# A selective-scan, attention and feed-forward kernel: the back stage's transposes, D*u, mean and the projection's z, put together in another way

## The chip, the cores and the metric

The kernel runs on one core of one Trainium2 chip. A core has TensorE (PE in the profile, with its weight loads as PEld), VectorE (DVE), ScalarE (ACT), GpSimd (POOL) and SyncE (SP), whose queue issues all of this kernel's DMAs. The metric is the device time of one execution in microseconds. Three runs of the kernel before gave 11664.7, 11660.78 and 11644.77 us; the median is 11660.78 us.

## The reference

The input is x, 8 images of 96 channels by 64 x 64 pixels (L = 4096). What is computed for each image:

```
xh  = layernorm over channels(x)
xz  = xh @ in_proj_w.T ;  xi, z = the two halves, 192 channels each
xi  = silu(depthwise 3x3 convolution(xi))
xs  = xi in four orders of the pixels (rows, columns, both reversed)
delta, B, C = projections of xs ;  A = -exp(A_log)
h_t = exp(delta_t*A)*h_(t-1) + delta_t*u_t*B_t ;  y_t = C_t.h_t + D*u_t
y   = sum of the four orders, back in pixel order
y   = layernorm over 192 channels(y) * silu(z)
out = y @ out_proj_w.T + x
```

After it come linear attention without a softmax (6 heads) and a feed-forward part with weights and activations rounded to eight bits. The layer norm over channels of the first line is (x - mean)/sqrt(var + 1e-5); the one of y is the one that the change rearranges.

## The kernel before

The images go in four pairs. Channels are on partitions; 4096 pixels are cut into 8 chunks of F = 512. The 192 channels are held as two halves of DIM = 96 (index g).

For every pair there are these stages, each a generator that gives control back with `yield`; `together` (line 880) interleaves two of them in program order:

- `project` (238): channel norm of x, then, per chunk, matmuls with winT: `pm` (128 channels of xi, line 287), `pl` (the other 64, written to the rows `lo` of image b, line 294) and `pz` twice (two halves of z, 96 channels each, line 303). ScalarE adds the bias into the padded images `y` (288, 295), and takes silu of z into `zt` (307), stored by one DMA to `zs` in DRAM (310).
- `convolve`, `gates`, `prepare` (313 to 439): the 3x3 convolution, silu, and the scan's inputs.
- `scan` (442): the recurrence, with an order of the instructions that is written out by hand (`manual_schedule`). Its results go to `ys` in DRAM.
- `back` (692): 16 chunks per pair (8 chunks of 2 images). For each: loads of z (`z3`, 731), u (`ut`, 733), x (`xr`, 738) and of the four orders of y (`yk`, 744 and 750, six DMAs, 1.5 MB); two adds that fold four orders into two (754 on VectorE, 755 on GpSimd); the transposes; the norm of y; the gate with z (796, 799); the output projection `po` (802) plus x into `ta` (806), which is stored to `t1`. `heads` (703) takes `ta` of the chunk before: a norm (`ncp`, `nvp`, lines 680 and 684, `tn` 687), keys and values `pk` (712), and their products `pm` (721).
- `tail` (829): attention's output and the feed-forward part.

`back` of one pair runs together with `project` of the next (16 steps against 34); for the last pair it runs alone. `tail` runs together with `convolve` and `prepare` of the next pair. `scan` runs by itself. Outside `scan`, the order in each engine's queue, SP's included, is set when the kernel is built, by the framework's planner, from program order, from buffers that come free and from its own estimates of durations. On the chip each engine takes its queue in order. Tile pools have a fixed number of buffers (`bk` 2, for yk, z3, ut, xr and others); a load waits until the buffer's last reader is done.

The scan leaves y with pixels on partitions, 24 channels (NE) side by side for each of 8 blocks, so a transpose on TensorE is a matmul with the data as weights and an identity as the moving operand. In `back`, half g of a chunk is put into the PSUM bank `py` in this way: first one matmul with `dpad[:, g]`, a diagonal with the sum of D, applied to u (line 759); then, for two orders k, four pixel groups j and four blocks e, one matmul each with 24 weight columns, written to rows 32e to 32e+23 (768). The channels so lie in four groups of 24 with 8 empty rows between. `py` is copied out to `yt` (773 on VectorE, 775 on ScalarE), and `c192` (identity minus the mean's 1/192, in the same padded layout) centres both halves with two matmuls each into two banks `yc` (781). ScalarE squares them (784), `j192` averages the squares into `yv` (788), and `rsqrt` is an Ln and an Exp on ScalarE (189, 190). Every float32 matmul appears as two matmul instructions in the profile.

Of the kernel before, what the change touches and what calls it, by code (L numbers as in the profile page):

```python
# [10 lines left out]
F32 = mybir.dt.float32  # L11
# [8 lines left out]
DIM = 96  # L20
# [32 lines left out]
def vss_attn_ffn(ctx: ExitStack, tc: tile.TileContext, a: dict):  # L53
# [26 lines left out]
    c192 = const.tile([128, 2, DIM], F32, name="c192")  # L80
    nc.vector.memset(c192, 0.0)
    for e in range(4):
        rows = slice(NE * e, NE * e + NE)
        nc.sync.dma_start(c192[32 * e : 32 * e + NE, 0], a["c192"][rows, 0, 0:DIM])
        nc.sync.dma_start(c192[32 * e : 32 * e + NE, 1], a["j192"][rows, 0, 0:DIM])
    nc.vector.tensor_scalar(c192[:, 1], c192[:, 1], -1.0, None, ALU.mult)
# [38 lines left out]
    inz = cut("inz", a["inb"][:, 1].unsqueeze(2), 1)  # L125
# [9 lines left out]
    dpad = const.tile([DIM, 2, 128], F32, name="dpad")  # L135
    nc.vector.memset(dpad, 0.0)
    for g in range(2):
        for e in range(4):
            nc.vector.tensor_scalar(
                dpad[:, g, 32 * e : 32 * e + NE], ident[0:DIM, NE * e : NE * e + NE],  # L140
                dsum[:, g : g + 1], None, ALU.mult,
            )
# [95 lines left out]
    def project(pair, zs, ybuf, p1, tmp, ps):  # L238
# [5 lines left out]
        nc.sync.dma_start(winT, a["winT"])  # L244
        for b in range(2):
# [36 lines left out]
            lo = slice(64 * b, 64 * b + 64)  # L282
            for c in range(NCH):
# [10 lines left out]
                nc.tensor.matmul(pl[lo], winT[:, 128:DI], xt[:, cs], start=True, stop=True)  # L294
# [5 lines left out]
                zt = tmp.tile([DIM, 2, F], F32, name="zt")  # L300
                for g in range(2):
                    pz = ps.tile([128, F], F32, name="pz", tag="fps")
                    nc.tensor.matmul(
                        pz[:DIM], winT[:, DI + g * DIM : DI + (g + 1) * DIM], xt[:, cs],
                        start=True, stop=True,
                    )
# [385 lines left out]
    def back(pair, ys, us, zs, t1, tn, tmp, psy, psc, psm, ps):  # L692
# [34 lines left out]
            for c in range(NCH):  # L727
                cs = bass.ts(c, F)
                for b in range(2):
                    zt = tmp.tile([DIM, 2, F], F32, name="z3")  # L730
                    nc.sync.dma_start(zt, zs[b, :, :, cs].rearrange("g p l -> p g l"))
# [22 lines left out]
                    nc.vector.tensor_tensor(yk[:, 0], yk[:, 0], yk[:, 2], ALU.add)  # L754
                    nc.gpsimd.tensor_tensor(yk[:, 1], yk[:, 1], yk[:, 3], ALU.add)  # L755
                    yt = tmp.tile([128, 2, F], F32, name="yt")
                    for g in range(2):
                        py = psy.tile([128, F], F32, name="py")
                        nc.tensor.matmul(py, dpad[:, g], ut[:, g], start=True, stop=False)  # L759
                        for k in range(2):  # L760
                            for j in range(4):
                                for e in range(4):
                                    o = py[32 * e : 32 * e + NE]
                                    if k % 2 == 0:
                                        o = o.rearrange("p (n j) -> p n j", j=4)[:, :, j]
                                    else:
                                        o = o.rearrange("p (g j w) -> p g j w", g=2, j=4)[:, :, j]
                                    nc.tensor.matmul(  # L768
                                        o, yk[:, k, 4 * g + e, NE * j : NE * j + NE], ident,
                                        start=False, stop=(k + j == 4),  # L770
                                    )
# [299 lines left out]
```

## Time and profile before

| | |
|---|---|
| median of three runs | 11660.78 us (11644.77 to 11664.7) |
| span of the profiled execution | 11664.0 us |
| TensorE busy | 8587.3 us (74%) |
| VectorE busy | 8817.1 us (76%) |
| ScalarE busy | 6931.4 us (59%) |
| GpSimd busy | 7968.6 us (68%) |
| DMA | 2095.89 MB, mean 180 GB/s |

The profile gives one execution. The page holds the busy time of each engine, the span in 40 slices, the DMA queues, the chain of work that ended last and the costliest groups of instructions. The trace answers more: the windows view gives each engine's busy time, the granted TensorE clock (1.00 is full) and the DMA share in any stretch; the timeline lists instructions in order of time; the groups view gives count, busy time and mean duration by line. The printed end of a matmul is modelled and has the depth of the pipeline in it.

### The profile page before, as it was taken

To read this page: it belongs to the slowest core of one execution; us is meant where nothing else is said; L and a number is where in the kernel's file an instruction comes from. 1 tells how busy PE (TensorE), PEld (TensorE's weight loads), DVE (VectorE), ACT (ScalarE), POOL (GpSimd) and SP (SyncE) were. 2 spreads that over 40 slices of the span, in tenths; PEclk is the share of its full clock that TensorE was granted. 3 is DMA by queue.
4 is the path that set the end of the run, shared out by engine and by line. 5 is a ranking of instruction groups with operands and counts; after the bars stand their busy time and mean duration, and the time that the engine had idled before them with its cause. 6 is when DMAs were issued, how large, how long until landed. Compare 5 with 4: busy or idle time off the path is not lost. (4 is left out here: it accounts for less than half of the span.)

```text
span 11664.0 us, 386998 instructions
## 1 busy us (share of the span) xinstructions
PE 8587.3 (74%) x170112; PEld 5661.1 (49%) x170112; DVE 8817.1 (76%) x6465; ACT 6931.4 (59%) x12227; POOL 7968.6 (68%) x2770
## 2 busy tenths in 40 slices
PE   7866666679876666767996666667898666666687
PEld 2255555554325555554422555555442355555542
DVE  5489999963659889995366999999445699999922
ACT  3666666654556666664455666666446566666623
POOL 0489999960259999994025999999303699999910
PEclk8678888889768888888976888888996688888896
DMA  2988888875488888886558888888636888888852
GB/s 82 233 200 203 197 200 200 199 165 135 134 200 198 198 191 199 205 198 152 125 152 203 198 198 201 199 202 199 148 98 181 205 202 203 201 194 200 191 133 65
DMA packets 1362204, 2095.89 MB, mean 180 GB/s; under 512 B 372484, under 2 KB 1012997, under 8 KB 1357701
## 3 DMA queue, kind: packets, MB, share of 16 engines
q1 hardware_dynamic: 1360516, 2071.13, 74.5%
q8 instruction: 1335, 21.87, 0.9%
q14 instruction: 353, 2.88, 0.1%
HBM read 1606.70 MB, written 464.01 MB: 178 GB/s over the span
## 5 line engine op out<-in xcount | busy, mean ns | idle before, releaser
L597 DVE TENSOR_TENSOR_SCAN h<-da,dbu 128x774 f32<-128x774 f32 x4096 | 7027.0, 1760 | 669.3 <-ACT da L586 449.9
L561 POOL TENSOR_TENSOR dbu<-dut,bc 128x1536 f32<-128x1536 f32 x2048 | 7084.1, 3508 | 615.6 <-ACT dbu L558 460.9
L586 ACT ACTIVATE da<-da 128x768 f32<-128x768 f32 x4092 | 3255.2, 798 | 2184.3 <-PE da L579 2145.6
L615 PE MATMUL yp<-h,cw 128*32 128x48 f32 x131072 | 3133.4, 246 | 1088.4 <-issue 1072.9
L579 PE MATMUL da<-dm,aw 128*128 128x128 bf16 x24576 | 2503.4, 251 | 1469.1 <-DVE h L597 1145.0
L615 PEld LDWEIGHTS yp<-h,cw 128*32 128x32 f32 x131072 | 2543.3, 155 | 1641.3 <-issue 1377.0
L579 PEld LDWEIGHTS <-aw 128*128 128x128 bf16 x24576 | 1844.6, 111 | 1785.9 <-issue 1467.5
L515 ACT ACTIVATE cw<-bc,blk 128x512 f32<-128x512 f32 x2048 | 1474.7, 721 | 251.0 <-DMA bc<-cs 222.1
L755 POOL TENSOR_TENSOR yk<-yk 128x768 f32<-128x768 f32 x64 | 117.2, 1831 | 1262.2 <-DMA yk<-ys 870.9
L433 POOL TENSOR_TENSOR dp<-rest,dp 128x512 bf16<-128x512 f32 x384 | 473.9, 1237 | 674.5 <-ACT dp L432 673.2
L623 ACT ACTIVATE yev<-yp 128x384 f32<-128x384 f32 x1024 | 503.4, 492 | 257.8 <-PE yp L615 256.8
L431 DVE TENSOR_TENSOR rest<-delta,dp 128x512 f32<-128x512 f32 x384 | 335.3, 876 | 420.4 <-ACT dp L430 420.2
L410 PE MATMUL pq<-S,dtw 12*128 12x512 f32 x768 | 559.0, 837 | 111.2 <-ACT delta L414 92.6
L796 DVE SCALAR_TENSOR_TENSOR g<-yc,c_onw,yrs 96x512 f32<-96x512 f32 x128 | 89.9, 742 | 472.1 <-ACT yrs L190 472.1
L868 POOL TENSOR_TENSOR ot<-t,y 96x512 f32<-96x512 f32 x64 | 101.8, 1590 | 483.7 <-DVE y L866 391.2
L558 ACT COPY dbu<-h 128x12 f32<-128x12 f32 x1984 | 407.9, 206 | 0.0
L432 ACT ACTIVATE dp<-rest 128x512 bf16<-128x512 f32 x384 | 240.2, 628 | 276.5 <-DVE rest L431 275.8
L410 PEld LDWEIGHTS pq<-S,dtw 12*128 12x128 f32 x768 | 155.2, 238 | 497.0 <-ACT delta L414 270.8
L682 ACT ACTIVATE nsq<-ncp 96x512 f32<-96x512 f32 x128 | 75.7, 592 | 523.6 <-PE ncp L680 496.8
L390 POOL COPY u<-xi 128x512 f32<-128x512 f32 x96 | 100.0, 1054 | 350.6 <-ACT xi L356 296.6
L768 PEld LDWEIGHTS py<-ident,yk 128*24 128x24 f32 x8192 | 229.2, 107 | 224.4 <-issue 166.9
L768 PE MATMUL py<-ident,yk 128*24 128x128 f32 x8192 | 311.9, 286 | 28.3 <-DVE yk L754 22.0
(136 smaller groups left out, 6764.8 us busy)
## 6 DMA issues: line engine op xcount, KB each, us to landing
dut<-du SPq DMA_DIRECT2D x1024, 768.0 KB
dm<-dl SPq DMA_DIRECT2D x512, 576.0 KB
dl<-dp SPq DMA_DIRECT2D x256, 384.0 KB
dm<-dl SPq DMA_DIRECT2D x512, 192.0 KB
ys<-yev SPq DMA_DIRECT2D x1024, 96.0 KB
du<-du SPq DMA_DIRECT2D x256, 256.0 KB
bc<-bs SPq DMA_DIRECT2D x512, 128.0 KB
bc<-cs SPq DMA_DIRECT2D x512, 128.0 KB
```

What stands on the lines that cost most here:

```text
L410: nc.tensor.matmul(pq, dtw[64:76, k, T], S[64:76], start=True, stop=True)
L431: nc.vector.tensor_tensor(rest, d, dp[:, :, 0], ALU.subtract)
L433: nc.gpsimd.tensor_tensor(dp[:, :, 2], rest, dp[:, :, 1], ALU.subtract)
L515: nc.scalar.activation(cw[i % 2][:, :, :, m, :].rearrange("p z j t -> p (z j) t"), bc[i][:, 1].rearrange("p z (j t) -> p (z j) t", j=NB), ...
L558: nc.scalar.copy(start, segs(hs[s - 1][:, :, r])[:, :, :, 1 if back else TC])
L561: nc.gpsimd.tensor_tensor(segs(t)[:, :, :, 1:], dut[g // 2][:, NI * (r % 2) : NI * (r % 2) + NI, :].unsqueeze(1) .to_broadcast([128, 2, NI ...
L579: nc.tensor.matmul(e[:, i], aw[k, r][:, i, z, :], dm[s // 2][:, NI * r + i, bass.ts(c % 2, TC)], start=True, stop=True,)
L586: nc.scalar.activation(e, e, AF.Exp)
L597: nc.vector.tensor_tensor_scan(hs[s][:, w, r][:, d], da[p % 3][:, o : o + W6][:, d], dbu[4 * s + r][:, w][:, d], 0.0, ALU.mult, ALU.add,)
L615: nc.tensor.matmul(y[32 * q : 32 * q + 32, 2 * NE * i : 2 * NE * i + 2 * NE] .rearrange("p (j r i) -> p i j r", j=2, r=NR), w[:, z, :, t], ...
L623: nc.scalar.activation(yev[s][:, :, o : o + 8, :].rearrange("p j i e -> p i j e"), y[:, 0 : 16 * NE].rearrange("p (i j e) -> p i j e", j=2 ...
L768: nc.tensor.matmul(o, yk[:, k, 4 * g + e, NE * j : NE * j + NE], ident, start=False, stop=(k + j == 4),)
```

## The change

The edits, in words:

1. After the adds, which now write into a new tile `yd` in the order (k, j, block, channel), the 96 channels of a half lie side by side. One matmul with 96 weight columns replaces four with 24: 16 per chunk instead of 64. The channels come out on rows 0 to 95 with no gaps.
2. `dpad` goes. VectorE's scalar_tensor_tensor reads `py` from PSUM and writes `yt = u*dsum + py`, in place of the copies.
3. The mean of y is one pair of matmuls with `j192` into one bank `mean`; VectorE subtracts it from both halves of `yt` in place, and ScalarE squares `yt`. `c192` goes, and so do the small loads and VectorE instructions that made `c192` and `dpad` at the start.
4. In `project`, the first 64 channels of z ride with the 64 rows of `pl` in one 128-column matmul (for the second image by a small extra tile `swap` with the columns exchanged), and the other 128 channels are one `pz` matmul: three matmuls per chunk instead of four. `zt` is stored by two DMAs. `zs` is laid out [2, 192, L].
5. `py` has two banks instead of one, the centring's pool one instead of two.

```diff
             lo = slice(64 * b, 64 * b + 64)
+            hi = slice(64 - 64 * b, 128 - 64 * b)
+            mixed = swap if b else winT[:, 128 : DI + 64]
...
-                nc.tensor.matmul(pl[lo], winT[:, 128:DI], xt[:, cs], start=True, stop=True)
+                nc.tensor.matmul(pl, mixed, xt[:, cs], start=True, stop=True)
...
-                zt = tmp.tile([DIM, 2, F], F32, name="zt")
-                for g in range(2):
-                    pz = ps.tile([128, F], F32, name="pz", tag="fps")
-                    nc.tensor.matmul(
-                        pz[:DIM], winT[:, DI + g * DIM : DI + (g + 1) * DIM], xt[:, cs],
-                        start=True, stop=True,
-                    )
+                zt = tmp.tile([128, 2, F], F32, name="zt")
+                pz = ps.tile([128, F], F32, name="pz", tag="fps")
+                nc.tensor.matmul(pz, winT[:, DI + 64 :], xt[:, cs], start=True, stop=True)
+                for r, g, v in ((hi, 0, pl), (slice(0, 128), 1, pz)):
                     table("silu", lambda: nc.scalar.activation(
-                        zt[:, g], pz[:DIM], AF.Silu, bias=inz[:, g]
+                        zt[r, g], v[r], AF.Silu, bias=inz[r, g : g + 1]
                     ))
-                nc.sync.dma_start(zs[b, :, :, cs].rearrange("g p l -> p g l"), zt)
+                nc.sync.dma_start(zs[b, 0:64, cs], zt[hi, 0])
+                nc.sync.dma_start(zs[b, 64:DI, cs], zt[:, 1])
...
-                    nc.vector.tensor_tensor(yk[:, 0], yk[:, 0], yk[:, 2], ALU.add)
-                    nc.gpsimd.tensor_tensor(yk[:, 1], yk[:, 1], yk[:, 3], ALU.add)
-                    yt = tmp.tile([128, 2, F], F32, name="yt")
+                    yd = tmp.tile([128, 2, 4, 8 * NE], F32, name="yd")
+                    for k, eng in ((0, nc.vector), (1, nc.gpsimd)):
+                        eng.tensor_tensor(
+                            yd[:, k].rearrange("p j (s e) -> p s j e", s=8),
+                            yk[:, k].rearrange("p s (j e) -> p s j e", j=4),
+                            yk[:, k + 2].rearrange("p s (j e) -> p s j e", j=4), ALU.add,
+                        )
+                    yt = tmp.tile([DIM, 2, F], F32, name="yt")
                     for g in range(2):
                         py = psy.tile([128, F], F32, name="py")
-                        nc.tensor.matmul(py, dpad[:, g], ut[:, g], start=True, stop=False)
                         for k in range(2):
                             for j in range(4):
-                                for e in range(4):
-                                    o = py[32 * e : 32 * e + NE]
...
-                                    nc.tensor.matmul(
-                                        o, yk[:, k, 4 * g + e, NE * j : NE * j + NE], ident,
-                                        start=False, stop=(k + j == 4),
-                                    )
-                        if g == 0:
-                            nc.vector.tensor_copy(yt[:, g], py)
-                        else:
-                            nc.scalar.activation(yt[:, g], py, AF.Copy)
-                    yc = []
+                                o = py[:DIM]
...
+                                nc.tensor.matmul(
+                                    o, yd[:, k, j, DIM * g : DIM * g + DIM], ident,
+                                    start=(k + j == 0), stop=(k + j == 4),
+                                )
+                        nc.vector.scalar_tensor_tensor(
+                            yt[:, g], ut[:, g], dsum[:, g : g + 1], py[:DIM], ALU.mult, ALU.add
+                        )
+                    mean = psc.tile([128, F], F32, name="mean")
+                    for g in range(2):
+                        nc.tensor.matmul(
+                            mean[:DIM], j192, yt[:, g], start=(g == 0), stop=(g == 1)
+                        )
                     sq = tmp.tile([DIM, 2, F], F32, name="ysq", bufs=1)
                     for g in range(2):
-                        p = psc.tile([128, F], F32, name="yc")
-                        for i in range(2):
-                            nc.tensor.matmul(
-                                p[:DIM], c192[:, i ^ g], yt[:, i], start=(i == 0), stop=(i == 1)
-                            )
-                        nc.scalar.activation(sq[:, g], p[:DIM], AF.Square)
-                        yc.append(p)
+                        nc.vector.tensor_tensor(yt[:, g], yt[:, g], mean[:DIM], ALU.subtract)
+                        nc.scalar.activation(sq[:, g], yt[:, g], AF.Square)
...
-                            gt, yc[g][:DIM], onw[:, g], rs, ALU.mult, ALU.mult
+                            gt, yt[:, g], onw[:, g], rs, ALU.mult, ALU.mult
...
-                        pool("bk", 2), pool("bky", 1, space=PSUM), pool("bkc", 2, space=PSUM),
+                        pool("bk", 2), pool("bky", 2, space=PSUM), pool("bkc", 1, space=PSUM),
```

More of the change, by code (lines that the diff above doesn't have):

```diff
@@ L124, in vss_attn_ffn @@
     woT = cut("woT", a["woT"], DIM)
-    inz = cut("inz", a["inb"][:, 1].unsqueeze(2), 1)
+    inz = const.tile([128, 2], F32, name="inz")
+    for o in (0, 64):
+        nc.sync.dma_start(inz[o : o + 64, 0:1], a["inb"][0:64, 1, 0:1])
+    nc.sync.dma_start(inz[0:64, 1:2], a["inb"][64:128, 1, 0:1])
+    nc.sync.dma_start(inz[64:128, 1:2], a["inb"][0:64, 1, 1:2])
     outb = load("outb", [DIM, 1])
@@ L244, in project @@
         nc.sync.dma_start(winT, a["winT"])
+        swap = p1.tile([DIM, 128], F32, name="swap")
+        nc.sync.dma_start(swap[:, 0:64], a["winT"][:, DI : DI + 64])
+        nc.sync.dma_start(swap[:, 64:128], a["winT"][:, 128:DI])
         for b in range(2):
```

27 lines of the change are left out of this document (6 added, 21 removed).

## The prediction

> **What bounds the kernel now.** First I read the page's parts 1 and 2, then where the changed lines run, then who is late there. No engine fills the span (VectorE 76%, TensorE 74%): the span is four scans of about 1900 us, in which the changed lines do not run, and the stages between them. By first and last starts in the trace, the back stage beside the next pair's projection runs from 2514 to 2944, 5384 to 5818 and 8240 to 8671 us (three "merged" stages, some 430 us each), the back stage alone from 11100 to 11486, and the first projection alone from 47 to 219. The rest, tail, convolution, preparation and scans, has no changed line. So the question is what ends last in these five stretches. The view of windows, for a merged stage past its start and for the back stage alone (columns: length, then busy us of PE, PEld, DVE, ACT, POOL, then granted clock, DMA share, GB/s):
>
> ```profile
> 5457.00:5795.00 338.00, 325.37 (x2531) 153.39 (x2529) 106.99 (x154) 165.39 (x259) 23.51 (x13) 1.00 0.58 136
> 11205.00:11287.00 82.00, 72.18 (x694) 36.88 (x687) 22.41 (x31) 23.35 (x40) 7.21 (x4) 1.00 0.64 143
> ```
>
> TensorE is the bound of the merged stage: 325 of 338 us at full clock, while ScalarE has 49%, VectorE 32%, GpSimd 7% and the DMA engines 0.58. Alone, the back stage has TensorE at 88%: nearly the bound, with some chain in it. So the next view is the timeline of TensorE over one chunk of the back stage alone (start, us, line):
>
> ```profile
> 11318.23 1.72 PE L768 MATMUL py<-ident,yk 128*24 128x128 f32 x54
> 11319.88 3.67 PE L781 MATMUL yc<-yt,c 128*96 128x512 f32 x8
> 11323.39 1.94 PE L788 MATMUL yv<-ysq,j 96*96 96x512 f32 x4
> 11325.17 1.02 PE L759 MATMUL py<-ut,dpad 96*128 96x512 f32 x2
> 11326.12 1.07 PE L768 MATMUL py<-ident,yk 128*24 128x128 f32 x32
> 11328.87 1.96 PE L802 MATMUL po<-g,c_woT 96*96 96x512 f32 x4 [1.67 <-DVE g L799]
> ...
> 11331.61 0.84 PE L768 MATMUL py<-ident,yk 128*24 128x128 f32 x18
> 11332.38 1.10 PE L684 MATMUL nvp<-nsq,c_j 96*96 96x512 f32 x2
> 11333.41 0.63 PE L768 MATMUL py<-ident,yk 128*24 128x128 f32 x14
> 11334.84 1.13 PE L759 MATMUL py<-ut,dpad 96*128 96x512 f32 x2 [0.80 <-DVE yt L773]
> 11335.90 0.40 PE L768 MATMUL py<-ident,yk 128*24 128x128 f32 x2
> 11336.23 1.57 PE L712 MATMUL pk<-c_wkv,tn 97*128 97x192 f32 x8
> ```
>
> The printed length of a group has the pipeline's end in it, so I cost a group from its start to the next group's start. The period is 20.86 us (the x54 group returns at 11339.09). In it are 3.51 us of L781, 0.95 + 1.06 of L759, and 128 instructions of L768 in 1.65 + 1.07 + 0.77 + 0.63 + 0.33 and 0.35 (a group of 8 at 11338.23) = 4.80 us. Two waits are visible: 1.67 us for the gate's g, and 0.80 us because the one py bank is still being copied out. The last view is the same timeline in the merged stage, at the projection:
>
> ```profile
> 5569.58 1.07 PE L294 MATMUL pl<-xt,winT 96*64 96x512 f32 x2
> 5570.59 1.13 PE L759 MATMUL py<-ut,dpad 96*128 96x512 f32 x2
> 5571.55 1.88 PE L303 MATMUL pz<-xt,winT 96*96 96x512 f32 x4
> 5573.27 1.88 PE L802 MATMUL po<-g,c_woT 96*96 96x512 f32 x4
> ```
>
> **The change, part by part, in TensorE's time per chunk of 512 pixels.**
>
> D*u through dpad goes: 2.01 us (in the merged stage 2 x 0.96 = 1.92). Four pairs of centring matmuls become one pair for the mean: half of 3.51 goes, 1.76. z in two matmul pairs becomes one: 1.72 us for four instructions, so 0.86 goes. The x matmul with 64 columns takes 1.01 against 0.95 for the 128-column one ahead of it (L287, 5568.63 to 5569.58), so widening it to carry 64 rows of z costs nothing and may give 0.06.
>
> The transposes are the unknown. Now 128 instructions take 4.80 us, 37 ns each; after, there are 32 with 96 weight columns and 128 moving columns, which no row has. The floor is the moving stream: L721 (128x96 weights, 96 moving) starts eight in 0.84 us less a 0.25 us end, 84 ns each, so 128 columns need 112 ns and 32 of them 3.6 us. The upper bound is L712 with 192 moving columns, 1.49 us for eight, 186 ns, 6.0 us. So the change is between -1.2 and +1.2 us; I take the gain of 1.2, since L721 has the same weights. The row's 37 ns is the price of 24 columns, and one instruction now does the work of four, 149 ns at that price. [...]
>
> VectorE gets more: two scalar_tensor_tensor out of PSUM and two subtractions with PSUM, minus one copy (687 ns). The nearest rows, of the same forms and sizes:
>
> ```profile
> L806 DVE SCALAR_TENSOR_TENSOR ta<-po,c_outb,xr 96x512 f32<-96x512 f32 x64 | 47.7, 745 | 102.6 <-PE po L802 102.6
> L687 DVE TENSOR_TENSOR tn<-ncp,nrs 96x512 f32<-96x512 f32 x64 | 43.8, 685 | 99.7 <-ACT nrs L190 97.3
> ```
>
> 2 x 745 + 2 x 685 - 687 = +2.2 us a chunk, 35 us a stage: VectorE goes from 107 to about 135 us in the window above, still far under TensorE; at zero cover it would be 2.2 us a chunk. ScalarE loses one copy (597 ns). The two adds now write in another order: 958 ns on VectorE, 1803 on GpSimd, both with idle time (75 and 215 us in eleven chunks) ahead of them; even doubled they stay under the period. SP's queue gets one more zs store per projection chunk (317 ns) and two small loads per pair, and is otherwise waiting (99.5 us for g between 11220 and 11440); eight small loads and nine VectorE instructions go from the start.
>
> On the chain: before, copy 0.69, four matmul pairs 3.51, square. After, 0.75, one pair 1.76, two subtractions 1.37, square. 4.2 against 3.9 us, so the chain of one chunk stays as long, and only overlap of chunks turns TensorE's saving into time. What helps is that yk is free once the adds have read it (now the transposes hold it), so its DMA can be issued a chunk earlier, and two py banks remove the 0.80 wait. What is late next is the new wait from mean to yv: subtraction and square, about 1.7 us with semaphores, which the next chunk's transposes can fill; if the planner puts po or the heads' ncp behind yv instead, they wait with it, and ta and z behind them.
>
> Merged stages: 1.92 + 1.76 + 0.86 + 1.2 = 5.7 us a chunk, 92 us a stage if all of it shows. The first three chunks run with half clock and waiting for yk; I give them 2 us each and the other thirteen 5.7: 80 us. Three stages: 240. Back stage alone: 2.01 + 1.76 + 1.2 = 5.0, plus 0.8 for the wait, minus 1.5 for the new one: 4.3 a chunk, 16.5 us instead of 20.86; four first chunks at 3: 64 us. First projection: 16 x 0.86 = 14, but the first half is followed by a VectorE that waits for the decay weights (DVE L230 to 129.4 us), so 7, and 2 for the start. Sum 240 + 64 + 9 = 313 us. The profiled span is 11664.0 us; its run was 11664.7 if it is the slowest of the three, and the median is 3 us less. 11661 - 313 = 11348.
>
> **The rivals.**
>
> (a) Half the saving is kept: the chain or a queue becomes the bound. SP issues in order, and z for chunk c+2 waits for g of chunk c (11329.50), with yk behind it; its last add ends 17 us later (11346.4), and g follows its transposes by 24 us; that loop of two chunks is 41 us, today's two periods. If the planner leaves yk behind z and TensorE's order does not tighten, the back stage alone gains 20 us; merged, where adds are ready 1 to 12 us before their transposes, 45 each: 160 us, 11500. For it: the nearly closed loop. Against it: 24 us of the loop contain the removed work.
>
> (b) Slower: the clock. TensorE at half clock, here as in the tail. Windows of 3.4 us (columns as above):
>
> ```profile
> 11283.90:11287.32 3.42, 1.78 (x4) 0.73 (x5) 2.25 (x4) 0.00 (x0) 0.00 (x0) 1.00 0.02 3
> 11512.50:11515.90 3.40, 2.72 (x5) 0.97 (x5) 0.00 (x0) 0.95 (x2) 0.00 (x0) 0.50 0.07 25
> ```
>
> A window with 52% busy is followed by one at 0.50 clock (11287.32), and in the tail 80% busy at half clock stays there. With less to do, TensorE falls under that share more often. A merged chunk of 25.3 us holds 19.6 of work afterwards; it is slower when over 5.7/19.6 = 29% of it runs at half clock. If all did, 3 x 13 x 13.9 = 540 us would be lost. Against it: 3.5 us of transposes and up to 7 us of matmuls in a row refill a window, and 100% windows bring the clock back (11290.73). [...]
>
> (c) No change: the stages end by something other than TensorE. Only if DMA bound: merged share 0.58 of 25.3 us is 14.7 us of transfers a chunk, under the 19.6 left; not believed.
>
> **How the numbers follow.** Forecast 11348 with 0.75; (a) 11500 with 0.15; (b) 0.07; (c) 0.03. Within the likeliest, the ends are transposes at 3.4 us and no start loss (5.9 a chunk: 3 x 95 + 16 x 5.2 + 16 = 384 saved, 11277) and transposes at 6.0 us (2.4 us x 64 = 154 less, 11502). The range 11270 to 11490 leaves out (b), (c), a part of (a) and the corner. 0.2% (23 us) is about what a measurement of this kernel can tell from no change: faster 0.90, same 0.03, slower 0.07.
>
> **What would show it.** Merged stages of about 350 us and the lone back stage of about 320; L768's successor with 2048 instructions about 110 ns apart; TensorE still over 90% busy in the merged stage at clock 1.00; yk issued before z of the same chunk. Wrong if the transposes start over 150 ns apart, if the granted clock shows 0.50 windows inside the merged stage, or if VectorE or yk's landing ends TensorE's waits there.

## The result, and the profile after

The changed kernel takes 11719.33 us (median of 12 runs, 11680.15 to 11735.12) against 11674.48 us for the kernel before, measured beside it (12 runs, 11637.27 to 11703.72): a ratio of 1.0037, 95% interval 1.0025 to 1.0050. It is slightly slower; the forecast was 11348 us. The profiled execution of after has a span of 11704.5 us against 11664.0.

TensorE is busy 8337.3 us where it was 8587.3: its busy time did fall, by 250 us. Why did the span not follow? The view of windows, laid over the second merged stage and the lone back stage, from the first z load to the stage's last matmul, to within 2 us (columns: length, busy us of PE, PEld, DVE, ACT, POOL, granted clock, DMA share, GB/s). Before:

```profile
5387.20:5819.50 432.30, 391.73 (x2898) 185.15 (x2899) 134.21 (x204) 186.71 (x292) 43.28 (x24) 0.93 0.58 133
11102.80:11483.60 380.80, 317.26 (x2696) 158.43 (x2696) 95.98 (x136) 95.67 (x160) 31.89 (x20) 0.90 0.56 125
```

After:

```profile
5368.20:5814.50 446.30, 336.77 (x1202) 180.64 (x1203) 168.68 (x252) 178.66 (x276) 45.53 (x24) 0.84 0.57 128
11114.30:11523.70 409.40, 295.27 (x1032) 159.96 (x1032) 126.80 (x184) 86.78 (x144) 30.80 (x20) 0.77 0.54 116
```

Read length minus the PE column as TensorE's idle time. Merged: 40.6 us became 109.5, +69. Alone: 63.5 became 114.1, +51. And read the clock column: 0.93 became 0.84, 0.90 became 0.77. Summing the trace's records of the granted clock, TensorE stood at half clock for 143 us of the merged stage (60 before) and 188 us of the lone one (73 before). That gives this account. Its first term is the forecast's own; the second is what is missing between it and the measured fall of the busy time; the third is measured:

| us | merged stage | lone stage |
|---|---|---|
| work removed, by the rows of the forecast (5.7 and 5.0 x 16) | -92 | -80 |
| given back: busy time fell by 55 and 22 only, as more of it ran at half clock | +37 | +58 |
| more idle time of TensorE | +69 | +51 |
| sum | +14 | +29 |

The sum comes out by construction. What checks the account is that the 37 and 58, found as a difference, come near half of the added half-clock time (82 and 114 us). Three merged stages and the lone one lose some 76 us by the stage lengths below, the first projection gains 29; the span grew by 40.5.

What TensorE waits for is told by the view of waits (total us, times, longest). For the gate's g ahead of po, in the steady part of the merged stage, after (5447 to 5785 us) and then before (5457 to 5795 us):

```profile
PE po L795 <- DVE g L792: 53.3, 14, 5.1
PE po L802 <- DVE g L799: 0.5, 1, 0.5
```

In the lone stage the same wait comes to 58.0 us where before had 32.8, and the new wait from mean to yv to 23.1. In neither steady part does TensorE wait for a load or for yd.

The timeline of TensorE shows both terms at work in one chunk of the lone stage (start, us, line; in brackets the idle time before and what ended it):

```profile
11300.28 1.96 PE L781 MATMUL yv<-ysq,j 96*96 96x512 f32 x4 [1.44 <-ACT ysq L778]
11305.87 3.70 PE L795 MATMUL po<-g,c_woT 96*96 96x512 f32 x4 [3.63 <-DVE g L792]
11309.36 1.91 PE L672 MATMUL ncp<-ta,c_c 96*96 96x512 f32 x2
11311.96 2.02 PE L676 MATMUL nvp<-nsq,c_j 96*96 96x512 f32 x2 [0.68 <-ACT nsq L674]
11313.77 2.82 PE L763 MATMUL py<-ident,yd 128*96 128x128 f32 x16
...
11324.18 1.96 PE L781 MATMUL yv<-ysq,j 96*96 96x512 f32 x4 [1.44 <-ACT ysq L778]
```

In the kernel before, a D*u matmul and 16 of the next chunk's transposes stand between yv and po (x32 instructions at 11326.12 in the forecast's timeline), and transposes fill the gaps of ncp and nvp too. Here po stands directly behind yv, and all transposes behind ncp and nvp. So TensorE waits out the chain of one chunk: 1.44 us for the subtraction and square, 3.63 for the gate, 0.68 for the heads' square. After the 3.63 us, the four instructions of po last 3.70 us where they took 1.96, and ncp and nvp are doubled as well (1.91 and 2.02 us where they took 1.02 and 1.10). The clock's part, in two windows of 3.41 us that meet where the trace's record of the clock falls:

```profile
11301.97:11305.38 3.41, 0.27 (x1) 0.00 (x0) 1.73 (x3) 1.31 (x2) 0.00 (x0) 1.00 0.84 139
11305.38:11308.80 3.42, 2.93 (x4) 1.23 (x5) 1.01 (x2) 0.00 (x0) 0.00 (x0) 0.50 0.00 0
```

The first window lies in the wait for g: TensorE is busy 8% of it. Then the clock stands at half for 10.24 us, three such windows, of which the last is filled; it comes back at 11315.62, in the middle of the transposes. The period of a chunk is 23.9 us (11300.28 to 11324.18) where it was 20.86.

The prices of the forecast, in contrast, are found again. The groups view of the lone stage (x is count; busy us, mean ns; idle time before, and what ended it):

```profile
L767 DVE SCALAR_TENSOR_TENSOR yt<-ut,dsum,py 96x512 f32<-96x512 f32 x18 | 13.4, 744 | 36.1 <-PE py L763 34.9
L777 DVE TENSOR_TENSOR yt<-yt,mean 96x512 f32<-96x512 f32 x18 | 11.5, 680 | 10.7 <-PE mean L772 10.7
```

744 and 680 ns were costed at 745 and 685. Sixteen of the transposes' instructions (half a chunk's) take 1.75 us at full clock to the next group's start (the timeline of the run lead5, below, 11199.85 to 11201.60), 109 ns each where the forecast had 112. No price was wrong enough to matter; the order was.

### The profile page after: what moved, and what is told of

Read it like the earlier page. It is cut to its first block, busy times and chain, and to the rows that moved or that the text cites. A ratio compares the mean times of both kernels' runs of the same rounds, so it can differ in the third digit from the quotient of the medians.

```text
span 11704.5 us, 373634 instructions
## 1 busy us (share of the span) xinstructions
PE 8337.3 (71%) x163328; PEld 5618.6 (48%) x163328; DVE 8950.0 (76%) x6646; ACT 6898.6 (59%) x12163; POOL 7979.4 (68%) x2770
## 5 line engine op out<-in xcount | busy, mean ns | idle before, releaser
L571 PE MATMUL da<-dm,aw 128*128 128x128 bf16 x24576 | 2471.4, 249 | 1447.0 <-DVE h L589 1147.2
L748 POOL TENSOR_TENSOR yd<-yk 128x768 f32<-128x768 f32 x64 | 123.5, 1930 | 1375.9 <-DMA yk<-ys 1138.3
L795 PE MATMUL po<-g,c_woT 96*96 96x512 f32 x256 | 220.2, 1011 | 238.3 <-DVE g L792 238.3
L763 PEld LDWEIGHTS py<-ident,yd 128*96 128x96 f32 x2048 | 280.1, 186 | 169.2 <-issue 126.4
L763 PE MATMUL py<-ident,yd 128*96 128x128 f32 x2048 | 287.0, 297 | 72.9 <-DVE yd L748 54.0
```

What stands on the lines that cost most here:

```text
L571: nc.tensor.matmul(e[:, i], aw[k, r][:, i, z, :], dm[s // 2][:, NI * r + i, bass.ts(c % 2, TC)], start=True, stop=True,)
L763: nc.tensor.matmul(o, yd[:, k, j, DIM * g : DIM * g + DIM], ident, start=(k + j == 0), stop=(k + j == 4),)
L795: nc.tensor.matmul(po[:DIM], woT[:, g], gt, start=(g == 0), stop=(g == 1))
```

## The experiments

Every run has its own measurement of the kernel before beside it (medians 11693.09 us for proj, t96, fill4 and pin_pe, 11703.92 for pin, pinb, a_cen and a_nodu, 11692.94 for lead5 and lead2, 11695.98 for lead2f and lead5f), so the ratios are what compares between rows. The stages here count from the end of the scan to the stage's last matmul (10 us more than from the first z load, as the forecast and most expectations count; lead2 and lead5 load yk before z, so for them only this count compares). In brackets: us of it at half clock.

| run | median us | ratio to before, 95% | three merged stages | lone back stage |
|---|---|---|---|---|
| before | - | 1 | 438 (55), 443 (67), 440 (61) | 391 (77) |
| after | 11719.33 | 1.0037 [1.0025, 1.0050] | 454 (150), 457 (149), 457 (153) | 420 (191) |
| proj | 11659.80 | 0.9969 [0.9953, 0.9984] | 436 (67), 437 (69), 436 (68) | 388 (71) |
| t96 | 11670.33 | 0.9979 [0.9965, 0.9994] | 432 (67), 432 (67), 429 (60) | 404 (121) |
| fill4 | 11607.22 | 0.9930 [0.9909, 0.9950] | 424 (62), 429 (71), 427 (65) | 370 (46) |
| pin_pe | 11549.25 | 0.9881 [0.9858, 0.9904] | 406 (99), 410 (103), 407 (96) | 363 (110) |
| pin | 11561.17 | 0.9883 [0.9865, 0.9901] | 409 (98), 410 (106), 408 (96) | 368 (140) |
| pinb | 11683.58 | 0.9985 [0.9973, 0.9997] | 433 (58), 435 (66), 431 (62) | 394 (101) |
| a_cen | 11650.19 | 0.9956 [0.9939, 0.9974] | 436 (109), 438 (114), 435 (101) | 383 (130) |
| a_nodu | 11765.82 | 1.0057 [1.0038, 1.0076] | 452 (125), 449 (118), 454 (129) | 424 (192) |
| lead2 | 11666.95 | 0.9968 [0.9953, 0.9983] | 442 (166), 438 (157), 435 (148) | 380 (137) |
| lead2f | 11627.88 | 0.9939 [0.9922, 0.9956] | 442 (76), 438 (62), 438 (69) | 376 (46) |
| lead5 | 11475.57 | 0.9814 [0.9796, 0.9831] | 400 (90), 401 (100), 402 (105) | 312 (56) |
| lead5f | 11461.55 | 0.9804 [0.9789, 0.9819] | 400 (93), 400 (86), 399 (89) | 317 (57) |

The theory from the profile after: the edits are worth their rows, but the order that the planner now chooses leaves the chain of one chunk open on TensorE, and the clock doubles the loss. The rivals: VectorE's new chain is the cost; the edits are worth nothing; the loads are the bound.

**One part alone: the projection (proj).** The kernel before with the projection's edit.

```diff
-                nc.tensor.matmul(pl[lo], winT[:, 128:DI], xt[:, cs], start=True, stop=True)
+                nc.tensor.matmul(pl, mixed, xt[:, cs], start=True, stop=True)
...
+                pz = ps.tile([128, F], F32, name="pz", tag="fps")
+                nc.tensor.matmul(pz, winT[:, DI + 64 :], xt[:, cs], start=True, stop=True)
```

> The projection's edits alone (three matmuls per chunk instead of four, two zs stores), the back stage as before. Theory 'order': the loss comes from the back stage, where the next chunk's transposes now stand behind po in TensorE's queue, so TensorE waits for the gate and its clock falls. Then this kernel keeps the gain that the first projection shows in the trace of after (first scan at 587 instead of 616 us) and takes up to 16 x 0.86 = 14 us off each merged stage: 11600 to 11650 us. Rival 'projection': the 128-row matmuls or the split store cost in the merged stage; then a merged stage is over 432 us and the total 11660 or more.

Measured 0.9969: this part is a gain, and most of it is not where the forecast had it. (11660 us is 10 us above the theory's range, beside a kernel before of 11693.) The first scan starts at 589.5 us instead of 615.6, 26 us earlier, where 9 were forecast; the merged stages gain 2 to 6 us each. The first projection in a window of 20 us, before:

```profile
160.00:180.00 20.00, 17.74 (x21) 4.54 (x19) 10.21 (x9) 6.49 (x11) 0.00 (x0) 0.50 0.00 0
```

then proj:

```profile
160.00:180.00 20.00, 18.76 (x36) 7.52 (x35) 13.93 (x10) 14.19 (x23) 0.00 (x0) 0.84 0.21 62
```

Before stays at half clock to 208 us, proj to some 165 us (21 and 36 instructions in the same 20 us): 82 against 55 us of half clock between 80 and 220 us. The removed pair was being paid at double price (the four instructions of pz take 3.52 us in the kernel before, 173.62 to 177.14 us, where the forecast's row has 1.72), and the clock came back sooner. Why it came back sooner was not tried.

**One part alone: the transposes (t96).** The kernel before with the adds into yd and 96 weight columns; D*u and the centring stay matmuls, with the old banks. (A few small tiles have one buffer instead of two, for space.)

```diff
-                                for e in range(4):
-                                    o = py[32 * e : 32 * e + NE]
...
-                                        o, yk[:, k, 4 * g + e, NE * j : NE * j + NE], ident,
+                                    o, yd[:, k, j, DIM * g : DIM * g + DIM], ident,
```

> The 96-column transposes and the adds' new order alone; D*u by a matmul, centring by four matmul pairs, the PSUM banks and the projection as before. Theory 'order': half of the old interleaving is left (only D*u's matmul stands between yv and po), so TensorE's saving of 16 x 1.2 us a stage is partly eaten by waits: 11620 to 11690 us. Rival 'VectorE' (the four added VectorE instructions lengthen the chain and are the whole loss): none is here, so all of 4 x 19 = 77 us is gained, about 11600 us. Rival 'transposes' (96 columns cost more than 24 packed): over 11700 us.

Measured 0.9979. The merged stages gain some 9 us each, the lone stage loses 13 with 121 us at half clock instead of 77. In TensorE's queue of the lone stage the transposes are no longer between yv and po; one D*u matmul is left there. So the transposes' edit alone already changes the order, and only the stage without the projection's matmuls, which had nothing else to put there, pays for it.

**More work, less time (fill4).** The changed kernel with four matmuls between yv and po, which nothing reads.

```diff
+                    fill = psc.tile([128, F], F32, name="mean")
+                    for _ in range(4):
+                        nc.tensor.matmul(fill[:DIM], j192, sq[:, 0], start=True, stop=True)
                     rs = tmp.tile([DIM, F], F32, name="yrs")
```

> The kernel after, plus four matmuls per chunk of 512 columns between yv and po, into the mean's bank, whose result nothing reads: 64 x 3.4 = 219 us more TensorE work, put where TensorE waits 3.6 us for the gate. Theory 'clock': the wait lets the clock fall, and po, ncp, nvp and half the transposes then take double, some 5 us a chunk; with the wait filled the clock stays at 1.00, the back stage alone goes from 409 to 340 to 370 us, the merged stages to 410 to 445, total 11580 to 11690 us, faster than after in spite of more work. If the clock is a by-product that costs nothing, the total is 11720 to 11800 us.

0.9930: with 219 us more TensorE work (64 chunks x 3.4 us at full clock) it is 1.1% faster than the changed kernel and faster than before. The same places in its timeline:

```profile
11211.80 1.96 PE L781 MATMUL yv<-ysq,j 96*96 96x512 f32 x4 [1.44 <-ACT ysq L778]
...
11217.40 1.93 PE L798 MATMUL po<-g,c_woT 96*96 96x512 f32 x4 [0.20 <-DVE g L795]
```

The wait before po is 0.20 us instead of 3.63, po takes 1.93 us instead of 3.70, and the lone stage has 46 us at half clock instead of 191. This separates the clock from the wait: the chain from yv to po is as long as it was (5.6 us from start to start in both), and 30 us a merged stage and 50 us of the lone one come back through the clock alone. With the clock kept up, the change is a gain even in the planner's order.

**The order (pin_pe).** The changed kernel with the loop written one chunk ahead, and one dependency that fixes po's place on TensorE behind the next chunk's transposes.

```diff
+                if n + 1 < 2 * NCH:
+                    ahead = first(n + 1)
                 mean = psc.tile([128, F], F32, name="mean")
...
+                    if g == 0 and n + 1 < 2 * NCH:
+                        after(s, ahead[5])
```

> The kernel after with the loop of the back stage written one chunk ahead (loads, adds, transposes and D*u of chunk n+1 ahead of chunk n's mean) and one order forced in TensorE's queue: po of chunk n behind the transposes of chunk n+1. Same instructions. Theory 'order': the transposes fill the wait for the gate, TensorE is the bound again; back stage alone 320 to 350 us instead of 409, merged 360 to 400 instead of 446: 11450 to 11580 us. Rivals 'VectorE' or 'transfers' (the chain through VectorE, or yk's landing, is the bound in any order): 11680 us or more.

0.9881: with the same instructions 1.6% faster than the changed kernel, and faster than the kernel before. The order explains the loss. The loop one chunk ahead and the dependency were not tried apart. It does not yet reach the forecast; TensorE now waits for yd:

```profile
11179.15 1.99 PE L773 MATMUL py<-ident,yd 128*96 128x128 f32 x16 [3.09 <-DVE yd L756]
```

**The same order on the kernel before (pinb).** The loop one chunk ahead and the same dependency, in the kernel before.

```diff
+                if n + 1 < 2 * NCH:
+                    ahead = first(n + 1)
                 yc = []
...
+                    if g == 0 and n + 1 < 2 * NCH:
+                        after(s, ahead[3])
```

> The kernel before with the same order as pin_pe: the loop is written one chunk ahead, and po of chunk n stands behind all transposes of chunk n+1 (64 of 24 columns and the two D*u matmuls). No part of the change is in it. Theory 'the edits are worth their rows, if the order keeps TensorE supplied': before already had 16 of its transposes between yv and po, so the order adds little or takes something (one py bank): 11620 to 11720 us, ratio to before 0.995 to 1.004, and pin_pe stays at least 70 us faster with the 5 us a chunk of removed work. Rival 'pin_pe is faster through the order alone, and the edits are worth nothing': pinb comes to 11549 plus or minus 25 us as well.

0.9985: next to nothing. So the order is not a gain of its own, the kernel before had one nearly as good; pin_pe is 1.0% faster than pinb, about 120 us, and that is what the edits are worth under one order. The rival that they are worth nothing falls.

**Which edit loses the order (a_cen, a_nodu).** The changed kernel with the centring by matmuls and the PSUM banks as before (a_cen), and with D*u by matmul (a_nodu).

```diff
-                        nc.vector.tensor_tensor(yt[:, g], yt[:, g], mean[:DIM], ALU.subtract)
-                        nc.scalar.activation(sq[:, g], yt[:, g], AF.Square)
+                        nc.scalar.activation(sq[:, g], p[:DIM], AF.Square)
```

> The changed kernel with the centring done by matmuls as before (four pairs into two banks, py with one bank), so that VectorE subtracts nothing and the wait from mean to yv is gone; D*u stays on VectorE, the transposes have 96 columns. Four matmul pairs in place of one add 1.76 us of TensorE a chunk. In TensorE's order po still stands directly behind yv. Theory 'place in the queue and clock': the wait of po for g stays and the half-clock windows with it; the subtraction's wait is taken by matmuls: 11640 to 11720 us, the lone back stage 385 to 410 us. Rival 'the new chain of subtractions on VectorE made it slower': the 1.4 us a chunk come back in full and the four stages with them, 11560 to 11620 us.

```diff
+                        nc.tensor.matmul(py[:DIM], dpad[:, g], ut[:, g], start=True, stop=False)
...
-                        nc.vector.scalar_tensor_tensor(
-                            yt[:, g], ut[:, g], dsum[:, g : g + 1], py[:DIM], ALU.mult, ALU.add
-                        )
```

> The changed kernel with D*u as a matmul again (96 columns, 1.92 us of TensorE a chunk) and copies out of PSUM in place of VectorE's multiply-add; mean and subtraction stay. In TensorE's order the two D*u matmuls of the next chunk come to stand between mean and yv, and po stays directly behind yv. Theory 'place in the queue and clock': more TensorE work in a wait costs nothing there and lifts the busy share, the wait for g before po stays: 11650 to 11720 us, less time at half clock than the 143 and 188 us of the changed kernel. Rival 'rows as in the forecast': 64 x 1.92 = 123 us more than the changed kernel, 11820 us.

Both miss their theory in a part. a_cen's median of 11650 us lies inside the theory's range, but beside a before of 11704; its lone stage of 372 us from the first z load is below both 385 and the kernel before's 381. Its timeline shows why no single reading can be taken from it:

```profile
11313.00 2.76 PE L799 MATMUL po<-g,c_woT 96*96 96x512 f32 x4 [3.63 <-DVE g L796]
...
11330.16 1.04 PE L766 MATMUL py<-ident,yd 128*96 128x128 f32 x8
11333.86 3.19 PE L799 MATMUL po<-g,c_woT 96*96 96x512 f32 x4 [2.66 <-DVE g L796]
```

The wait for the subtraction is gone, as meant, but in every other chunk some transposes also came to stand between yv and po. The mean's wait and the order changed together, so how much the subtraction on VectorE costs by itself stays open; that it is the whole cost is excluded by pin_pe, which has it and is faster. a_nodu is 0.2% slower than the changed kernel, about 23 us for 123 us of added TensorE work (the two intervals overlap, so the 23 us are not clear of noise): the half-clock time of the merged stages falls by some 27 us each, so part of the work was hidden and part was not. The forecast's row for that part (1.92 us a chunk saved) was worth a fifth of its price in this order, or less.

**More places in the order (pin).** As pin_pe, with VectorE's second operation for g behind the next add, and the t store behind the next yk loads.

```diff
+                    if g == 0 and n + 1 < 2 * NCH:
+                        after(s, ahead[4])
...
+                if n + 1 < 2 * NCH:
+                    after(s, ahead[3])
```

> The changed kernel with the transposes of chunk n+1 ahead of po of chunk n (as in the run pin_pe), and two more places in the order fixed: VectorE's second operation for g stands behind the next chunk's add, and the t store stands behind the next chunk's yk transfers on SP's queue. In pin_pe's lone back stage TensorE still waits 3.08 us in nearly every chunk for VectorE's add (VectorE waits there for g first) and in the merged stages some 40 us in eleven chunks for yd on VectorE and GpSimd. Theory 'place in the queues': these waits go as well, 13 x 3 = 40 us alone and some 15 to 30 us in each merged stage: 11430 to 11500 us, with less time at half clock (under 70 us a stage instead of 92 to 103). Rival 'TensorE's work and the chain of one chunk are what is left': the time stays within 20 us of pin_pe's 11549 us, the waits only change their name.

No difference to pin_pe, but the run decides nothing: its edit moved almost nothing. The traces of pin and pin_pe have the same order in SP's queue, in the second merged stage and in the lone one, and in pin_pe VectorE's add stands ahead of g's second operation already. So the rival's figure held without a test of its reason. TensorE still waits for VectorE's add in 9 of 10 chunks, up to 3.1 us. The waits of SP's queue between 11100 and 11300 us (total, times, longest):

```profile
SPq L731 <- DVE g L814: 73.9, 10, 7.8
SPq L824 <- DVE ta L823: 40.1, 10, 5.6
```

VectorE's add stands behind g's first operation, which waits for the norm. GpSimd's add of the same chunk starts some 1.3 us after it, with 18 to 19 us of idle time before it that end, by the trace, with the ut load, issued right behind the chunk's yk loads; so an earlier place for VectorE's add alone should give little, which was not tried. And the six yk loads of a chunk are spread over SP's queue between a z load that waits for g, a t store that waits for ta and a tn store that waits for tn. This looks like the loop of rival (a), come up once the order on TensorE is mended; no run took it alone.

**Loads two chunks ahead, and two orders on TensorE (lead2, lead5).** Both issue the yk loads two chunks ahead and fix them before the t store, and both put VectorE's work for the next chunk before g. They differ in TensorE's order, as the expectations say.

```diff
+                    yk = nxt[0]
+                    nxt = fetch(n + 2) if n + 2 < 2 * NCH else None
...
+                    s, add = turn(yd, yn, own[1], 0, s)
...
+                    s = heads2(*late, s)
+                if more:
+                    tr, st = turn(yd, yn, own[1], 1, s)
```

> As lead5 with the yk loads two chunks ahead and before the t store, but on TensorE the simpler order po(n-1), ncp, nvp, pk, pm, mean(n), yv(n), all transposes of n+1, po(n): the wait of po is filled, those of nvp, pk and yv are not (0.7 + 2.6 + 1.4 us a chunk). Theory 'the edits are worth their rows once the order keeps TensorE supplied and the loads early': lone back stage 300 to 330 us by 12.6 + 4.7 + 1 us a chunk, merged stages 365 to 395 us, 11420 to 11500 us. Rival 'the loads are the loop that is left': stages within 15 us of pin_pe's 397 and 352 us.

> The changed kernel's instructions in another order. The yk loads go two chunks ahead and stand before the t store; on TensorE the order is po(n-1), mean(n), ncp, nvp, half of the transposes of n+1, yv(n), pk, pm, the other half, po(n), so that each wait of the chain of one chunk has other matmuls in it; VectorE's multiply-add for n+1 stands before g of n. Nothing is added or left out. By the rows a chunk has 12.6 us of TensorE work alone and 19.6 beside the projection, and some 2.5 us of short waits are left in it. Theory 'the edits are worth their rows once the order keeps TensorE supplied and the loads early': lone back stage 260 to 300 us, merged stages 340 to 375 us with less than 70 us at half clock, 11300 to 11430 us, which is where the forecast of 11348 us was. Rival 'the loads, by SP's queue or by the DMA engines, are the loop that is left': stages within 15 us of pin_pe's 397 and 352 us, 11500 to 11560 us, with TensorE waiting for yd whose adds wait for yk.

lead5: 0.9814, 2.2% faster than the changed kernel; 11476 us is 46 us above its theory's range and below its rival's. A chunk of its lone stage:

```profile
11196.98 1.10 PE L672 MATMUL ncp<-ta,c_c 96*96 96x512 f32 x2
11198.92 1.10 PE L678 MATMUL nvp<-nsq,c_j 96*96 96x512 f32 x2 [0.84 <-ACT nsq L676]
11199.85 1.91 PE L791 MATMUL py<-ident,yd 128*96 128x128 f32 x16
11201.60 1.88 PE L834 MATMUL yv<-ysq,j 96*96 96x512 f32 x4
...
11210.82 1.93 PE L857 MATMUL po<-g,c_woT 96*96 96x512 f32 x4 [0.24 <-DVE g L854]
11213.59 1.10 PE L672 MATMUL ncp<-ta,c_c 96*96 96x512 f32 x2 [0.84 <-DVE ta L863]
```

The period is 16.6 us, at full clock in this chunk; the forecast had 16.5 us for the changed kernel. The lone stage gains 79 us on the kernel before, where 64 were forecast. The merged stages gain 40 each, not 80. Their time is no longer lost in the steady chunks but at two places, in windows of 50 us:

```profile
5331.00:5381.00 50.00, 27.11 (x325) 19.49 (x326) 10.55 (x14) 3.45 (x6) 17.88 (x9) 0.65 0.91 176
...
5431.00:5481.00 50.00, 46.60 (x188) 24.40 (x187) 25.53 (x36) 26.69 (x42) 3.64 (x2) 1.00 0.64 144
...
5531.00:5581.00 50.00, 36.15 (x140) 18.71 (x139) 25.69 (x35) 16.72 (x27) 5.41 (x3) 0.83 0.84 189
```

At the start and in the middle the DMA engines are 91% and 84% busy and TensorE has 27 and 36 of 50 us of work at a lowered clock; between them it has 46.6 at full clock. The kernel before has the first of the two as well (28.2 us of work in its first 50 us, 5377 to 5427) but not the second (48.0 of 50 us, 5577 to 5627).

lead2 missed. It has the loads early and most of po's wait filled, and yet its merged stages are as long as before, with as much half-clock time as the changed kernel (148 to 166 us):

```profile
11156.22 1.10 PE L676 MATMUL nvp<-nsq,c_j 96*96 96x512 f32 x2 [0.68 <-ACT nsq L674]
11159.47 2.64 PE L704 MATMUL pk<-c_wkv,tn 97*128 97x192 f32 x8 [2.16 <-DVE tn L679]
...
11166.66 1.96 PE L813 MATMUL yv<-ysq,j 96*96 96x512 f32 x4 [1.44 <-ACT ysq L810]
```

Three waits of 0.68, 2.16 and 1.44 us lie within 11 us here, and pk takes 2.64 us, much of it at half clock: the clock falls at 11159.80, after a window in which TensorE was busy 1.25 of 3.41 us.

**Filling what is left (lead2f, lead5f).** Unread matmuls in those three waits (six a chunk), and in lead5's waits of ncp and nvp (two a chunk).

```diff
+            nc.tensor.matmul(vp[:DIM], j96, src_, start=True, stop=True)
...
+                    for _ in range(3 if n == 0 else 0):
+                        m = nc.tensor.matmul(pk[:DIM], j96, ta, start=True, stop=True)
```

> As lead2, with six more matmuls of 512 columns in every chunk whose results nothing reads: one in the wait of nvp for the square (0.68 us), three in the wait of pk for tn (2.16), two in the wait of yv for the square (1.44); 0.86 us each, 5.2 us a chunk, 330 us more TensorE work in all. lead2 missed its 365 to 395 and 300 to 330 us (it has 413 to 420 and 358 us, with 119 to 147 us a stage at half clock). Theory 'clock': those three waits, close together, bring windows under half busy; filled, the stages come to at most 70 us at half clock and fall to 375 to 405 and 310 to 345 us, 11500 to 11620 us, though TensorE has 330 us more to do. Rival 'lead2 is slow because of its chain or its loads': the same stages or longer by up to 1 us a chunk, 11665 to 11730 us.

> As lead5, with two more unread matmuls of 512 columns a chunk, one in the wait of ncp for ta (0.84 us) and one in the wait of nvp for the square (0.68 us): 1.7 us a chunk, 110 us more TensorE work. lead5's merged stages still have 74 to 86 us at half clock (lone 41). Theory 'clock': the merged stages come to at most 55 us at half clock; each loses 10 to 25 us of half-clock work and pays up to 6 us for matmuls that are longer than their waits, so 11420 to 11465 us. Rival 'lead5's half-clock time is the stage's start and its middle, where loads are late, not these waits': half-clock time stays, and the time is 11475 to 11520 us.

lead2f: the half-clock time falls as expected, to 46 to 76 us, but the stages keep their length, and the time (0.9939 against 0.9968) hardly moves: here 330 us of added work and the regained clock nearly cancel, and 11628 us lies between the theory's range and the rival's. In fill4 the fill (3.4 us) was shorter than the wait (3.63), here each fill is longer than its wait (0.9, 2.6 and 1.7 us for 0.68, 2.16 and 1.44). That suggests, on two runs, that filling pays where the fill is the shorter. lead5f: the same as lead5 within the interval, half-clock time down by at most 16 us a stage. Its median, 11462 us, lies in the theory's range, but the half-clock time that the theory needed (at most 55 us) did not come. As its rival said, what is left in lead5 is the stage's start and its middle, not these short waits. Whether the loads alone set those two places was not tried.

## Why the prediction was wrong, point by point

- **The step that failed: "the chain of one chunk stays as long, and only overlap of chunks turns TensorE's saving into time", with the overlap then taken as given.** The next step named the risk: "the new wait from mean to yv ... which the next chunk's transposes can fill; if the planner puts po or the heads' ncp behind yv instead, they wait with it". It did; the forecast priced that wait at 1.5 us a chunk of the lone stage, and nothing in the merged one. Measured: 1.44 us for that wait, and 3.63 us for g before po, where before had 1.67. The sum has no term for the second, which is the larger: the new wait was priced, but not what the removed matmuls and the moved transposes had covered (58.0 us against 32.8 in the lone stage, 53.3 against 0.5 in 338 us of the merged one). The idle time rose by 69 and 51 us a stage. pin_pe, with the same instructions in another order, is 1.6% faster than the changed kernel.
- **Rival (b), the clock, had 0.07 and was the other half.** The reason given against it, that "3.5 us of transposes and up to 7 us of matmuls in a row refill a window", assumed the old order. With the waits open, a merged stage has 143 us at half clock and the lone one 188. It did not decide alone: it gave back 37 and 58 us of the 92 and 80 saved, the waits 69 and 51; with either mended alone (fill4, pin_pe) the change is a gain. The forecast's own sign of being wrong, 0.50 windows inside the merged stage, could not tell by itself, as the kernel before has 60 us of them there. The chunk above has a wait of 3.63 us, in it a window 8% busy, and then the drop. The clock also fell after windows that were 52% busy (the forecast's own, 11283.90) and 37% (lead2, 11159.80). What busy share brings the drop no run took alone.
- **Rival (a), SP's loop,** was not what happened first. It may be the bound that shows next, as SP's queue holds the yk loads behind stores that wait; but pin could not test it, and lead5 changed the loads and the order together, so that stays open.
- **The prices held.** Transposes 109 ns each (112 forecast), multiply-add 744 ns (745), subtraction 680 (685). Four instructions of 24 columns took some 150 ns together (37 each), the one of 96 in their place takes 109.
- **Merged stages, 80 us forecast:** lost 16; with the order of lead5, 40 gained. With that order the mis-sized term is the gain a chunk, 5.7 us in thirteen chunks. In the second merged stage po follows po after 24.0 us in the kernel before (mean of thirteen steps; 21.1 to 26.0 once the stage runs, where the forecast took 25.3 from one stretch) and after 19.8 in lead5: 4.3 us saved. The other two steps, near the start and in the middle, take 38 and 39 us where before had 31 and 23; that loss of 23 us has no term in the sum.
- **Lone stage, 64 us forecast:** lost 29; with lead5, 79 gained at the forecast period (16.6 against 16.5 us).
- **First projection, 9 us forecast:** 29 gained in the changed kernel, 26 in proj. The saved matmuls ran at half clock there, and the row they were priced from was at full clock.

## What to carry to other kernels

When an edit takes work away from the engine that is the bound, ask what stood in that place of its queue: small independent instructions that filled a wait are worth their cover as well as their time. Where a planner sets the order from its own costs, compare the order of the queues of the two kernels before adding up rows, and fix the places that matter (here a loop written one chunk ahead and one dependency were worth 1.6%). Where the trace shows TensorE's clock fall behind a wait of a few us, price that wait twice: its length, and the instructions after it at half clock (here three windows of 3.41 us after one wait of 3.63, and po at 3.70 us where it took 1.96).

## What the runs showed of the hardware that was not expected

- Adding matmuls saved time in fill4: 219 us more of them made the changed kernel 1.1% faster, as the clock stayed up (62 to 71 us at half clock in a merged stage for 149 to 153, 46 in the lone one for 191). 330 us more in lead2 cost nothing that was measured (0.9939 against 0.9968).
- The clock also fell behind windows in which TensorE was half busy. In the trace of the kernel before it changes in steps of 3.41 us. In the 3.41 us ahead of its 588 drops TensorE was busy 45% (median; 50% or less in three of four). Of the windows after which the clock stayed at full, none was under 48%.
- It came back after fuller windows: in the same trace those that end a stretch at half clock were busy 93% or more in nine of ten, 77% at the least (the stretch at the span's end not counted). Not each full window was followed by it: of the 622 other windows of such stretches 91 were 100% busy. In the changed kernel's chunk above, one wait of 3.63 us has three windows at half clock behind it, and TensorE in lead2, with waits of 0.68, 2.16 and 1.44 us a chunk, was at half clock for over a third of its merged stages (166 of 442, 157 of 438 and 148 of 435 us).
